# Layer-norm statistics from x's blocks instead of loaded rows, short steps moved between VectorE and GpSimd, three score visits a group, in a fused pre-norm attention kernel

## The chip, the cores and the metric

The kernel runs on one NeuronCore of one Trainium2 chip. The metric is device time in microseconds (us), the median over runs of the whole program. The engines are called as the profile calls them: PE is TensorE's matmul, PEld its weight load, DVE is VectorE, ACT ScalarE, POOL GpSimd, SP the queue that issues the DMAs. Each engine works through its own queue strictly in the order in which the kernel wrote its instructions, and waits on semaphores where one needs another's result.

## What is computed

One layer of graph attention with a layer norm ahead of it, in fp32, for 128 graphs of 128 nodes with 768 features, 12 heads of 64:

```
h = relu((x - mean(x)) / sqrt(var(x) + 1e-5))          # over the 768 features
q, k, v = h@Wq + bq, h@Wk + bk, h@Wv + bv              # 768 x 768 each, split in 12 heads
scores = q @ k.T / 8 + beta * adj
scores = where(adj > 0, scores, -9e15)
out = x + merge_heads(softmax(scores) @ v)
```

About one entry in eight of adj is positive.

## The kernel before

**Groups and slices.** The 128 graphs go in 32 groups of 4. A group's projections come in three slices: `qk0` (q and k of the first six heads), `v`, and `qk1` (q and k of the other six). Group 0 computes them plainly. From group 1 on each slice is a fast matrix multiplication of a 2x3 by a 3x3 block matrix in 15 block products instead of 18 (the table `PRODUCTS`). Its left factors are the normalized activations, transposed (`A00` to `A12`), and ten sums of them (`S0` to `S14`, in `SUMS_A`); its right factors are weight blocks and sums of these, prepared once in group 0, stored in HBM, and streamed in again in every group through a ring of six tiles (`load_T`), except ten that stay resident. Each of the 45 products of a group is 14 matmuls of 128x64 by 128x128 in pairs (28 instructions in the trace, line 681).

**Banks, evictions, decodes.** PSUM is held as four pairs of banks. The 15 products of a slice form four chains (a to d): a chain takes one pair for all its products and accumulates in it, and its running sum is added into the result tiles after each product (`evict`, DVE, line 704; the first addition to a tile goes mostly over ACT, lines 716 and 724 to 726, since it also brings the bias). The next product of a chain waits for the eviction before it, and the pair is given back after the chain's last one. When a result tile has all its parts, `decode` (lines 739 to 742 for q and k, 750 to 754 for v) turns its seven blocks into the four wanted. A decode runs on POOL or on DVE as the table `DECODE` says.

**Attention.** For each pair of heads (`oc`, 0 to 5) there are: `scores` (64x64-tiled matmuls, line 776, into a pair of its own), `mask` (DVE, 789), `exp` (ACT, 798), `attend` (matmuls of 65 columns, line 855), `drain` (ACT, 885 and 887), `recip` (DVE, 824), `divide` (ACT, 836), `add` of the residual (904; DVE, but POOL for three of the last group's), and `send`. `attend` puts its matmuls one by one between those of the next product. A time at which PE leaves the products for one or more scores is called a visit here.

**Layer norm of a later group.** The group's four graphs are loaded twice. The first time row by row (`load_row`, 384 KB each, with nodes on partitions): ACT sums each row (521), scales it (522) and sums the squared deviations (523), DVE and POOL make the inverse deviation and the shift from that (530, 534, 535), and both go to HBM and come back in the block order (`turn_out` 539, `turn_in` 543). The second time x is loaded in blocks (`load_x`, 295), 32 nodes of a quarter of the features on each quarter of the partitions; ACT normalizes the blocks (`norm`, 560), DVE transposes them into the left factors (`to_hT`, 580), POOL completes these (`inner`, 590 to 592), DVE makes the ten sums (`sum_acts`, 585).

**Order.** From group 1 on the order is written out: one unit is the place of a product, 45 units are a group. `ORDER` gives the order of a slice's products, `EVICT` and `DECODE` the keys of evictions and decodes, `TABLE` those of all else (relative to the group whose work it is; negative keys lie in the group before). `slice_z` issues a product and then everything whose key lies below the next unit. Separate tables hold for the first groups (`FIRST`, `SECOND`) and the last (`LAST`). Two scores whose keys lie in the same unit are thus one visit.

Of the kernel before, what the change touches and what calls it, by code (L numbers as in the profile page):

```python
# [11 lines left out]
F32 = mybir.dt.float32  # L12
# [6 lines left out]
P = 128  # L19
# [13 lines left out]
def kernel(  # L33
# [77 lines left out]
ZORDER = (1, 0, 5, 2, 3, 7, 10, 11, 6, 13, 4, 9, 14, 8, 12)  # L111
QORDER = (4, 0, 1, 8, 2, 3, 5, 6, 7, 10, 9, 11, 13, 12, 14)
VORDER = (1, 0, 5, 3, 2, 10, 6, 7, 13, 4, 11, 9, 8, 12, 14)
LORDER = (1, 4, 0, 5, 8, 2, 3, 10, 6, 7, 13, 11, 9, 14, 12)
PORDER = (1, 0, 5, 2, 3, 10, 7, 6, 13, 11, 4, 9, 14, 8, 12)
XORDER = (1, 0, 5, 2, 3, 10, 6, 7, 13, 11, 4, 9, 14, 8, 12)
ORDER = {"qk0": (1, 0, 5, 2, 10, 3, 6, 7, 13, 11, 9, 4, 14, 12, 8), "v": (1, 0, 5, 2, 10, 3, 6, 7, 13, 11, 4, 9, 14, 8, 12), "qk1": (4, 1, 0, 8, 2, 5, 3, 6, 7, 10, 9, 13, 11, 12, 14)}
RING = 6
RESIDENT = (10, 12, 16, 21, 29, 33, 36, 39, 41, 42)
# [6 lines left out]
    (-103.105, 'row', 0), (-86.74, 'row_stats', 0), (-85.688, 'row', 1), (-78.233, 'row_stats', 1),  # L126
    (-76.202, 'row', 2), (-71.584, 'row_stats', 2), (-67.928, 'row', 3), (-64.453, 'row_stats', 3),
    (-54.853, 'moments'), (-53.424, 'load_x', 0, (0,)), (-50.853, 'load_x', 0, (1,)), (-49.522, 'powers'),
    (-51.725, 'load_x', 0, (2,)), (-49.052, 'turn_out'), (-49.398, 'load_x', 0, (3,)), (-46.515, 'turn_in'),
    (-40.942, 'norm', 0, 2, 4), (-41.357, 'norm', 0, 0, 2), (-40.317, 'norm', 1, 2, 4), (-39.199, 'norm', 1, 0, 2),  # L130
    (-37.336, 'turn', 'A01'), (-34.768, 'turn', 'A02'), (-35.86, 'turn', 'A00'), (-33.123, 'load_x', 1, (0,)),
    (-32.146, 'load_x', 1, (1,)), (-30.708, 'load_x', 1, (2,)), (-32.534, 'load_x', 1, (3,)), (-24.763, 'inner', 'A00'),
    (-24.393, 'norm', 2, 0, 2), (-25.315, 'norm', 2, 2, 4), (-23.262, 'norm', 3, 2, 4), (-23.244, 'norm', 3, 0, 2),
    (-23.578, 'inner', 'A01'), (-20.844, 'adj'), (-18.417, 'inner', 'A02'), (-20.599, 'turn', 'A11'),
# [4 lines left out]
    (5.399, 'sum', 'S5'), (8.41, 'sum', 'S14'), (9.857, 'sum', 'S11'), (17.129, 'scores', 0, 2),  # L139
    (17.594, 'mask', 2), (18.011, 'exp', 2), (17.884, 'scores', 0, 1), (20.163, 'mask', 1),  # L140
    (23.187, 'exp', 1), (23.44, 'scores', 0, 0), (24.691, 'mask', 0), (26.808, 'xo', 2),
    (29.787, 'exp', 0), (33.304, 'attend', 2), (34.708, 'drain', 2), (38.169, 'recip', 2),
    (37.453, 'attend', 1), (40.226, 'divide', 2), (40.335, 'xo', 1), (40.001, 'drain', 1),
    (40.047, 'attend', 0), (42.314, 'xo', 0), (41.101, 'drain', 0), (41.291, 'recip', 1),
    (42.019, 'add', 2), (43.363, 'send', 2), (41.655, 'recip', 0), (47.272, 'xo', 5),
    (42.336, 'divide', 0), (46.026, 'divide', 1), (47.4, 'add', 1), (49.422, 'send', 1),
    (47.396, 'scores', 1, 2), (47.912, 'mask', 5), (47.949, 'scores', 1, 0), (49.895, 'add', 0),
    (49.151, 'mask', 3), (51.424, 'send', 0), (50.757, 'exp', 5), (51.214, 'scores', 1, 1),
    (51.428, 'mask', 4), (56.184, 'xo', 4), (50.986, 'exp', 3), (52.741, 'attend', 5),
    (53.334, 'drain', 5), (53.605, 'recip', 5), (54.069, 'divide', 5), (54.524, 'attend', 3),  # L150
    (55.36, 'drain', 3), (57.434, 'recip', 3), (54.287, 'xo', 3), (57.116, 'add', 5),
    (58.808, 'send', 5), (52.838, 'exp', 4), (58.432, 'divide', 3), (57.867, 'attend', 4),
    (58.283, 'drain', 4), (58.872, 'recip', 4), (61.984, 'divide', 4), (63.775, 'add', 3),
    (69.353, 'add', 4), (70.997, 'send', 4), (72.651, 'send', 3),
)
FIRST = (
    (47.506, 'scores', 1, 2), (48.607, 'mask', 5), (50.338, 'xo', 5), (51.293, 'exp', 5),
    (48.854, 'scores', 1, 0), (49.931, 'mask', 3), (53.115, 'exp', 3), (50.06, 'scores', 1, 1),
    (52.234, 'mask', 4), (52.147, 'xo', 3), (55.733, 'exp', 4), (52.181, 'attend', 5),
    (53.448, 'drain', 5), (54.046, 'xo', 4), (53.711, 'recip', 5), (55.811, 'divide', 5),  # L160
    (55.187, 'attend', 3), (56.589, 'drain', 3), (58.071, 'recip', 3), (60.187, 'add', 5),
    (58.585, 'divide', 3), (58.053, 'attend', 4), (59.743, 'drain', 4), (60.118, 'recip', 4),
    (64.402, 'send', 5), (62.463, 'divide', 4), (61.794, 'add', 3), (62.914, 'add', 4),
    (63.456, 'send', 3), (67.258, 'send', 4),
)
SECOND = (
    (-15.32, 'sum', 'S6'), (-45.161, 'halve'),
)
SOONER = (
)  # L170
LAST = (
    (35.303, 'xo', 0), (31.635, 'xo', 1), (26.501, 'xo', 2), (32.505, 'attend', 2),
    (33.547, 'drain', 2), (33.554, 'recip', 2), (35.3, 'divide', 2), (35.121, 'attend', 0),
    (36.619, 'drain', 0), (35.991, 'add', 2), (37.63, 'recip', 0), (40.956, 'send', 2),
    (38.462, 'divide', 0), (39.644, 'attend', 1), (40.439, 'drain', 1), (38.622, 'add', 0),
    (41.811, 'scores_half', 3, 1), (40.516, 'recip', 1), (41.663, 'send', 0), (40.926, 'divide', 1),
    (41.938, 'scores_half', 5, 0), (42.905, 'attend_half', 3, 1), (43.277, 'out_half', 3, 1), (41.384, 'add', 1),
    (42.934, 'attend_half', 5, 0), (44.439, 'scores_half', 5, 1), (43.462, 'out_half', 5, 0), (44.118, 'send', 1),
    (45.949, 'scores_half', 4, 0),
)  # L180
DECODE = {
# [45 lines left out]
def direct(ctx, tc, x, adj, wq, bq, wk, bk, wv, bv, beta, out, bad):  # L227
# [62 lines left out]
    def load_x(G, r, parts=range(NB)):  # L290
        if parts[0] == 0:
            home_x(G, r)
# [1208 lines left out]
```

## Time and profile before

| | before |
|---|---|
| median of 3 runs | 2666.85 us (2665.64 to 2668.2) |
| span of the profiled execution | 2664.1 us |
| PE busy | 2644.1 us, 99% |
| DVE, ACT, POOL busy | 81%, 66%, 79% |
| DMA | 736.65 MB, mean 277 GB/s |

A row of the timeline has the start in us from the span's start, the length, the engine, the line, and the operation with what it writes and reads; "x28" joins as many neighbours. As matmuls overlap, time on PE is read from start to start. In the groups by line a row ends with busy us, mean ns of one, and the idle time of the engine ahead of them with what ended it. "issue" is a wait for nothing that the profile shows.

### The profile page before, as it was taken

Reading aid. Unit: us, or ns where it says so; the run is one execution under the profiler, and the core shown is the slowest. Engines: PE = TensorE matmul, PEld = TensorE weight load, DVE = VectorE, ACT = ScalarE, POOL = GpSimd, SP = SyncE. Lnnn points to the kernel's source line nnn. Section 1 sums busy time; section 2 is a strip of 40 time slices with the busy share of each in tenths; the row PEclk is TensorE's granted clock in tenths of the full one; section 3 lists DMA queues with packets and bytes.
Section 4 is the critical chain, followed back from the end, with each engine's and each line's share of the span. In section 5 each row is a group of like instructions: output and inputs, shape, how many; then the busy total and the mean of one; then the engine's idle time right before and its main releaser. Section 6 shows DMA issues by size and latency. Waiting matters only on the chain.

```text
span 2664.1 us, 121442 instructions
## 1 busy us (share of the span) xinstructions
PE 2644.1 (99%) x52041; PEld 2564.2 (96%) x52041; DVE 2165.8 (81%) x2702; ACT 1755.1 (66%) x4608; POOL 2097.8 (79%) x3043
## 2 busy tenths in 40 slices
PE   9999999999999999999999999999999999999998
PEld 8799999999999999999999999999999999999997
DVE  7878887878888788887788887888877888778876
ACT  2567766677666677666777666776667776667654
POOL 5877778877779777788777797777887777887774
PEclk9999999999999999999999999999999999999999
DMA  8899999998989999999999899999899898999885
GB/s 254 276 281 279 282 284 278 283 292 267 293 281 279 287 277 284 281 281 280 289 269 288 281 281 282 288 275 285 279 278 292 268 291 279 276 286 282 256 253 165
DMA packets 531572, 736.65 MB, mean 277 GB/s; under 512 B 106444, under 2 KB 371160, under 8 KB 531032
## 3 DMA queue, kind: packets, MB, share of 16 engines
q1 hardware_dynamic: 530384, 728.06, 88.5%
q8 instruction: 411, 6.73, 1.0%
q14 instruction: 129, 1.06, 0.1%
q10 hardware_dynamic: 648, 0.79, 0.1%
HBM read 662.22 MB, written 66.51 MB: 274 GB/s over the span
## 4 chain that ended last, share of the span: by engine, by line
PE 94%; DVE 1%; DMA 0%; issue 0%; ACT 0%; SPq 0%; DVEq 0%; ACTq 0%
PE pair L681 80%; PE pair L776 7%; PE pair L855 6%; PE pair L1048 1%; DVE home L704 0%; DMA x<-in_x_dram 0%; DMA T_qk<-kept_qk 0%; PE pair L926 0%; DVE e L789 0%; DVE prep_qk L403 0%; ACT e L836 0%; DVE res_qk L403 0%; PE pair L947 0%; DVE e L931 0%; ACT e L933 0%
## 5 line engine op out<-in xcount | busy, mean ns | idle before, releaser
L704 DVE TENSOR_TENSOR home<-home,pair 128x896 f32<-128x896 f32 x836 | 880.0, 1077 | 220.5 <-PE pair L681 179.8
L681 PE MATMUL pair<-sbig,T_qk 128*64 128x128 f32 x13020 | 827.6, 274 | 2.3 <-DVE home L704 1.2
L681 PEld LDWEIGHTS pair<-sbig,T_qk 128*64 128x64 f32 x13020 | 702.5, 137 | 19.9 <-issue 12.1
L739 POOL TENSOR_TENSOR home<-home 128x256 f32<-128x256 f32 x308 | 266.1, 864 | 320.0 <-DVE home L704 319.7
L681 PE MATMUL pair<-T_v,sbig 128*64 128x128 f32 x7812 | 457.8, 273 | 1.6 <-ACT home L716 0.6
L681 PE MATMUL pair<-A,T_qk 128*64 128x128 f32 x6944 | 445.6, 273 | 0.9 <-issue 0.9
L681 PEld LDWEIGHTS pair<-T_v,sbig 128*64 128x64 f32 x7812 | 430.7, 137 | 8.4 <-ACT e L836 4.8
L855 PE MATMUL pair<-v,e 128*64 128x65 f32 x6048 | 403.5, 221 | 0.0
L836 ACT ACTIVATE e<-e,sm 128x64 f32<-128x64 f32 x1512 | 381.7, 341 | 7.4 <-DVE sm L824 6.1
L681 PEld LDWEIGHTS pair<-A,T_qk 128*64 128x64 f32 x6944 | 384.6, 137 | 1.5 <-issue 1.5
L855 PEld LDWEIGHTS pair<-v,e 128*64 128x64 f32 x6048 | 362.2, 137 | 3.2
L724 ACT ACTIVATE home<-pair 128x640 f32<-128x640 f32 x340 | 240.6, 708 | 188.5 <-PE pair L681 187.2
L681 PE MATMUL pair<-sbig,res_qk 128*64 128x128 f32 x4340 | 312.3, 273 | 0.4
L742 POOL TENSOR_TENSOR home<-home 128x256 f32<-128x256 f32 x308 | 269.7, 876 | 24.1
L885 ACT ACTIVATE sm<-pair,tiny 128x8 f32<-128x8 f32 x189 | 50.8, 269 | 329.5 <-PE pair L855 329.5
L789 DVE SCALAR_TENSOR_TENSOR e<-pair,biasT 128x1024 f32<-128x1024 f32 x189 | 229.4, 1214 | 34.1 <-PE pair L776 33.0
L740 POOL TENSOR_TENSOR home<-home 128x256 f32<-128x256 f32 x308 | 228.2, 741 | 24.1
L681 PEld LDWEIGHTS pair<-sbig,res_qk 128*64 128x64 f32 x4340 | 238.0, 137 | 1.4 <-DVE home L704 1.3
L560 ACT ACTIVATE x<-x,block 128x192 f32<-128x192 f32 x480 | 222.6, 540 | 0.0
L726 ACT ACTIVATE home<-pair,bqk 128x128 f32<-128x128 f32 x680 | 214.3, 377 | 0.0
L798 ACT ACTIVATE e<-e 128x1024 f32<-128x1024 f32 x189 | 196.1, 1055 | 21.8 <-DVE e L789 14.0
L741 POOL TENSOR_TENSOR home<-home 128x128 f32<-128x128 f32 x308 | 175.6, 570 | 24.2
(208 smaller groups left out, 4401.6 us busy)
## 6 DMA issues: line engine op xcount, KB each, us to landing
T_qk<-kept_qk SPq DMA_DIRECT2D x713, 448.0 KB
T_v<-kept_v SPq DMA_DIRECT2D x372, 448.0 KB
xo<-in_x_dram SPq DMA_DIRECT2D x190, 256.0 KB
out_dram<-xo SPq DMA_DIRECT2D x189, 256.0 KB
x<-in_x_dram SPq DMA_DIRECT2D x248, 192.0 KB
sbig<-in_x_dram SPq DMA_DIRECT2D x116, 384.0 KB
kept_qk<-prep_qk SPq DMA_DIRECT2D x23, 448.0 KB
adj<-in_adj_dram SPq DMA_DIRECT2D x128, 64.0 KB
```

The costliest lines, as they stand in the source:

```text
L560: nc.scalar.activation(t, t, AF.Relu, bias=shift[G, n], scale=rstd[G, n])
L681: nc.tensor.matmul(p[q:q + HD, at, :], lhs[:, q:q + HD], rhs, start=(first and at % 4 == 0), stop=True, skip_group_check=True)
L704: nc.vector.tensor_tensor(t, t, p[:, 0:7], op)
L724: nc.scalar.activation(t[:, 0:5], p[:, 0:5], AF.Copy, scale=float(sign))
L726: nc.scalar.activation(t[:, at], p[:, at], AF.Identity, bias=bqk[:, of, oc:oc + 1], scale=float(sign))
L739: e.tensor_tensor(t[:, 1:4:2], t[:, 1:4:2], twice(5), ALU.add)
L740: e.tensor_tensor(t[:, 2:5:2], t[:, 2:5:2], twice(1), ALU.add)
L742: e.tensor_tensor(t[:, 0:7:6], t[:, 0:7:6], twice(2), ALU.add)
L789: nc.vector.scalar_tensor_tensor(e[:, :, at], ps[:, :, at], SCORE_CAP * ISCALE, bias[:, :, at], op0=ALU.min, op1=ALU.add)
L798: nc.scalar.activation(e, e, AF.Exp, scale=1.0 / ISCALE)
L836: nc.scalar.activation(o[:, r, b, 0:HD], pa[:, r, b, 0:HD], AF.Copy, scale=t[:, 1, r, b:b + 1])
L855: nc.tensor.matmul(pa[q:q + HD, 2 * g + i, :], k[:, q:q + HD], vt[G, "v", r, h // 4][:, 4 * g + h % 4, :], start=True, stop=True, skip_gro ...
```

## The change

**Statistics from the blocks.** `load_row`, `row_stats`, `moments`, `turn_out` and `turn_in` go. For two graphs at a time (r = 0, 1), DVE runs `bn_stats` on the blocks of x that are loaded anyway, 16 steps of 128x192 a group; the results go to HBM and come back with all four quarters of a node's features on every partition that needs them; seven short DVE steps combine them (`comb`), POOL takes the power (`powers`), now twice a group with 8 columns.

```diff
+    def bn(G, g):
+        for b in range(NB):
+            nc.vector.bn_stats(st_x[:, (g % 2) * NB + b, :], xg[G, g][:, b, :])
+    def stout(G, r):
+        t = turned[G, r] = dram.tile([SQ, NB, 2 * NB * 6], F32, name=f"turned_{G}_{r}")
+        nc.sync.dma_start(t.rearrange("i a s -> a i s"), st_x.rearrange("p m s -> p (m s)"))
+    def stin(G, r):
+        nc.sync.dma_start(back.rearrange("p a m s -> p (a m s)"), turned.pop((G, r)).rearrange(
+            "i a s -> i (a s)")[None].to_broadcast([NB, SQ, NB * 2 * NB * 6]))
+    def comb(G, r):
+        v = back.rearrange("p a m (h s) -> p a m h s", h=2)
+        total = stat.tile([P, 2, 2 * NB], F32, tag="total", name=f"total_{G}_{r}", bufs=1)
+        nc.vector.tensor_reduce(total[:, 0], v[:, :, :, :, 1].rearrange("p a m h -> p m a h"), AX.XY, ALU.add)
+        nc.vector.tensor_scalar(total[:, 0], total[:, 0], -0.125, None, op0=ALU.mult)
+        nc.vector.tensor_tensor(dev, v[:, :, :, :, 1], total[:, 0][:, None, :, None].to_broadcast([P, NB, 2 * NB, 2]), ALU.add)
+        nc.vector.tensor_tensor(dev, dev, dev, ALU.mult)
+        nc.vector.scalar_tensor_tensor(dev, v[:, :, :, :, 2], 2.0 / QD, dev, op0=ALU.mult, op1=ALU.add)
+        nc.vector.tensor_reduce(total[:, 1], dev.rearrange("p a m h -> p m a h"), AX.XY, ALU.add)
+        nc.vector.tensor_scalar(total[:, 1], total[:, 1], 0.125, EPS, op0=ALU.mult, op1=ALU.add)
```

**Who does what.** Four of the ten sums and three of the six adds of a group move from DVE to POOL; four decodes a group are on DVE where one was. `OPEN` can give a first eviction to DVE in part (1) or whole (2); of its entries two meet a first eviction in the new order: `('v', 2): 1`, which cuts an ACT step in two, and `('qk1', 10): 1`, which gives three of seven blocks to DVE. Three attentions a group (`oc` 0, 2, 4) are issued in one piece, not between the matmuls of the next product.

```diff
+ADD_POOL = (1, 4, 5)
+SUM_POOL = ('S7', 'S11', 'S1', 'S9')
+WHOLE = (0, 2, 4)
 DECODE = {
+    ('qk0', 0, 0): (3.197731, 'v'), ('v', 0, 0): (8.0, 'v'), ('v', 1, 1): (4.200223, 'v'), ('qk1', 0, 0): (4.769773, 'v'),
...
-        nc.vector.tensor_tensor(t, full[G, a], full[G, b], ALU.add if sign > 0 else ALU.subtract)
+        e = nc.gpsimd if name in SUM_POOL and G > 1 else nc.vector
+        e.tensor_tensor(t, full[G, a], full[G, b], ALU.add if sign > 0 else ALU.subtract)
...
-        between.append(attend_steps(G, oc, behind))
+        steps = attend_steps(G, oc, behind)
+        if (G or oc > 2) and oc in WHOLE:
+            for _ in steps:
+                pass
+        else:
+            between.append(steps)
```

**Three visits and new tables.** All of `ORDER`, `RESIDENT`, `TABLE`, `EVICT`, `DECODE` and `LAST` has new keys; the fifteen products of a slice stay. `FIRST`, `SECOND` and the slots of group 0 give way to `EARLY` and to `TABLE` itself, whose keys count in group 1 too. Assertions (`needs`, `did`) now state at build time what must have been issued before what; they issue nothing.

```diff
-ORDER = {"qk0": (1, 0, 5, 2, 10, 3, 6, 7, 13, 11, 9, 4, 14, 12, 8), "v": (1, 0, 5, 2, 10, 3, 6, 7, 13, 11, 4, 9, 14, 8, 12), "qk1": (4, 1, 0, 8, 2, 5, 3, 6, 7, 10, 9, 13, 11, 12, 14)}
+ORDER = {'qk0': (4, 1, 0, 8, 5, 2, 3, 10, 6, 7, 9, 11, 13, 12, 14), 'v': (4, 1, 8, 5, 10, 0, 3, 2, 7, 13, 6, 11, 9, 14, 12), 'qk1': (4, 1, 0, 8, 3, 5, 2, 10, 6, 7, 9, 13, 11, 12, 14)}
 TABLE = (
-    (17.129, 'scores', 0, 2), (17.884, 'scores', 0, 1), (23.44, 'scores', 0, 0),
-    (47.396, 'scores', 1, 2), (47.949, 'scores', 1, 0), (51.214, 'scores', 1, 1),
+    (18.989782, 'scores', 0, 2), (18.992782, 'scores', 0, 1), (18.995782, 'scores', 0, 0),
+    (49.992037, 'scores', 1, 2), (49.995037, 'scores', 1, 0), (55.18473, 'scores', 1, 1),
...
+    (-29.538203, 'bn', 3), (-29.183478, 'stout', 1), (-29.137527, 'stin', 1),
+    (60.668615, 'attend', 3), (61.942528, 'attend', 4),
 )
```

More of the change, by code (lines that the diff above doesn't have):

```diff
@@ L346, in raw_qk1_piece @@
         v = flat(0, RAW).rearrange("p (c i n) -> p c i n", c=NC, i=2)
+        needs("part", "qk0", n=27)
+        did("raw")
         a, i = at // 2, at % 2
@@ L670, in product @@
             banks[chain] = take()
+        needs("A", G, an)
+        assert not waiting.get(chain)
+        waiting[chain] = len(uses)
         bank = banks[chain]
@@ L769, in scores @@
         oc = 3 * u + j
+        if G:
+            needs("decode", G, u, j, n=2)
         ps = take()
@@ L1007, in put, with slice_z @@
         heapq.heappush(events, (at, named[0], f, args))
-    def slice_z(G, sl, todo):
+    def slice_z(G, sl):
+        assert not prep
         order = order_of(G, sl)
         base = 45 * G + 15 * ("qk0", "v", "qk1").index(sl)
-        name = {(1, "qk0"): "first", (NG - 1, "v"): "vlast", (NG - 1, "qk1"): "last"}.get((G, sl), sl)
+        own = f"{sl}_last" if G == NG - 1 else f"{sl}_{G}"
         for k, n in enumerate(order):
@@ new lines, in direct, with placed @@
+        "raw": lambda G, n: raw_qk1_piece(n), "home": ninth_home, "load_T": lambda G: load_T(), "scores_half": scores_half, "attend_half": attend_first, "out_half": out_half,
+    }
+    for at, name, G, *args in EARLY:
+        put(at, actions[name], G, *args)
+    inputs = ("load_x", "bn", "stout", "stin", "comb", "powers", "norm", "turn", "inner", "adj", "bias1", "square", "bias2", "bias3")
+    def placed(G, at, name, args):
+        if name == "scores":
+            u = args[0]
+        elif name in ("mask", "exp", "xo", "attend", "drain", "recip", "divide", "add", "send"):
+            u = args[0] // 3
+        else:
+            if G == 1 and name in inputs:
+                return False
+            if G == 1 and name == "sum" and args[0] in ("S1", "S9", "S10", "S2", "S6"):
+                return False
+            return G > 0
+        if G == NG - 1:
+            return not u and name == "scores"
+        return G > 0 or u == 1
```

397 lines of the change are left out of this document (211 added, 186 removed), and 55 rows, old and new, of tables (DECODE, EVICT, OPEN, TABLE).

## The prediction

> **What bounds the kernel now.** I read the page first, then the busy time by windows, the chain of waits in order of time, and PE's timeline around the stretches that the change moves.
>
> ```profile
> span 2664.1 us, 121442 instructions
> ...
> PE 2644.1 (99%) x52041; PEld 2564.2 (96%) x52041; DVE 2165.8 (81%) x2702; ACT 1755.1 (66%) x4608; POOL 2097.8 (79%) x3043
> ```
>
> PE (TensorE) works through the whole span. A window of 82 us in the middle shows every engine's share there; its columns are length, PE, weight loads, DVE, ACT, POOL, granted clock, DMA share, GB/s.
>
> ```profile
> 918.00:1000.00 82.00, 82.00 (x1673) 80.40 (x1670) 67.49 (x81) 55.63 (x146) 66.34 (x96) 1.00 0.92 281
> ```
>
> PE has no hole, at full clock. DVE is busy 82%, POOL 81%, ACT 68%, the DMA engines 92%. Not one of them holds PE up. The chain of waits agrees: its longest pieces are one and the same piece of PE work, once a group.
>
> ```profile
> 252.99 15.65 PE pair L681 x284
> ...
> 334.02 15.65 PE pair L681 x284
> ...
> 2527.99 15.65 PE pair L681 x284
> ```
>
> The first two are 81.03 us apart, the shortest group. From the first to the last are 28 groups in 2275.0 us, 81.25 each: some 0.22 us a group, 6.2 us in all, are irregular waits. So there is next to nothing to win by relieving another engine. Only less work on PE counts, and the danger is that a busier engine makes PE wait.
>
> **Part by part: the PE stream.** The products are the same fifteen per slice, in another order. What changes is how often PE leaves them for scores.
>
> ```profile
> 211.69 1.98 PE L776 MATMUL pair<-home 64*64 64x128 f32 x64
> 213.59 4.81 PE L681 MATMUL pair<-sbig,T_qk 128*64 128x128 f32 x84
> 218.23 1.70 PE L681 MATMUL pair<-A,T_qk 128*64 128x128 f32 x28
> 219.86 0.67 PE L776 MATMUL pair<-home 64*64 64x128 f32 x16
> 220.34 0.62 PE L776 MATMUL pair<-sbig 64*64 64x128 f32 x16
> 220.89 1.86 PE L681 MATMUL pair<-sbig,T_qk 128*64 128x128 f32 x30
> ```
>
> Read start to start, since ends overlap. A visit with two scores (x64) lasts 213.59 - 211.69 = 1.90; one with a single score (x32) 220.89 - 219.86 = 1.03. A score more costs 0.87, so 0.16 of a visit is not for scores. The product ahead of the single visit lasts 219.86 - 218.23 = 1.63, where products elsewhere take 1.53:
>
> ```profile
> 1001.87 1.70 PE L681 MATMUL pair<-sbig,res_qk 128*64 128x128 f32 x28
> 1003.40 1.70 PE L681 MATMUL pair<-A,T_qk 128*64 128x128 f32 x28
> ```
>
> Another 0.10 is thus paid on entry: 0.26 us a visit, whatever it holds. Before, a group has four visits: keys 17.129 and 17.884 fall into one slot, 23.44 into another, 47.396 and 47.949 into one, 51.214 alone. After, 18.990 to 18.996 are one slot with three scores, 49.992 and 49.995 one, 55.185 alone: three. The first half's visit is saved in groups 1 to 31; in group 0 three visits of the second half become two. 32 x 0.26 = 8.3 us less on PE, the one term on the path. As bounds: 32 x 0.16 = 5.1 if entry is paid in any case, 8.3 if the third score is never late.
>
> Three of the six attentions are now issued whole, not between the products' matmuls. The last group has one that stands alone:
>
> ```profile
> 2644.34 0.93 PE pair L947 x32
> ```
>
> 0.93 us for 32 instructions. PE's stream holds those 32 either way, and nothing in this row suggests that standing together costs more: zero, with the neighbouring products as cover for its weight loads; without that cover the bound is the 0.10 of a change of shape, three times a group, 9 us in all.
>
> **Part by part: the other engines.** Prices, as busy time and mean of one:
>
> ```profile
> L704 DVE TENSOR_TENSOR home<-home,pair 128x896 f32<-128x896 f32 x836 | 880.0, 1077 | 220.5 <-PE pair L681 179.8
> ...
> L904 DVE TENSOR_TENSOR xo<-xo,e 128x512 f32<-128x512 f32 x186 | 161.8, 870 | 0.1
> ...
> L585 DVE TENSOR_TENSOR sbig<-sbig,A 128x896 f32<-128x896 f32 x93 | 118.5, 1274 | 1.0
> ...
> L534 POOL TENSOR_TENSOR row<-verow,nhalf 128x4 f32<-128x4 f32 x30 | 30.8, 1028 | 0.0
> ...
> L464 DVE BATCH_NORM_STATS2 st<-x 128x6 f32<-128x192 f32 x16 | 4.4, 343 | 2.6 <-DMA x<-in_x_dram 2.6
> ...
> L904 POOL TENSOR_TENSOR xo<-xo,e 128x512 f32<-128x512 f32 x3 | 3.6, 1185 | 9.1 <-ACT e L836 9.1
> ```
>
> A decode (four steps from L739 on) on DVE, start to start, and beside it a sum that met POOL at work:
>
> ```profile
> 1012.32 1.60 DVE L585 TENSOR_TENSOR sbig<-A,A 128x896 f32<-128x896 f32 x1
> ...
> 1018.84 0.65 DVE L739 TENSOR_TENSOR home<-home 128x256 f32<-128x256 f32 x1
> ...
> 1021.96 1.34 DVE L585 TENSOR_TENSOR sbig<-sbig 128x896 f32<-128x896 f32 x1
> ```
>
> 3.12 us. And two on POOL, the second beside that sum of 1012.32:
>
> ```profile
> 1010.09 0.73 POOL L739 TENSOR_TENSOR home<-home 128x256 f32<-128x256 f32 x1
> ...
> 1012.93 1.58 POOL L739 TENSOR_TENSOR home<-home 128x256 f32<-128x256 f32 x1
> ...
> 1017.14 0.72 POOL L739 TENSOR_TENSOR home<-home 128x256 f32<-128x256 f32 x1
> ```
>
> 2.84 us undisturbed, 4.21 where it meets DVE; I take 3.1, nearer the first.
>
> DVE per group: now 67.49 x 81.03 / 82 = 66.7. Added: 16 statistics steps at 4.4 / 16 = 0.275, 4.4; 14 short steps of the combination, between nothing beyond their issue and the 0.34 of a statistics step, I take 0.2, 2.8; three more decodes at 3.12 (a v decode priced like a qk one, an estimate), 9.4; half an eviction where the split puts three of seven blocks on DVE, 0.5. Gone: four sums at 1.27, 5.1; three adds at 0.87, 2.6. Net +9.4, 76.1 of the new period of 80.77: 94%. Bounds: 73.3 with the short steps free, 78.1 with all at 0.34.
>
> POOL per group: now 65.6. Gone: three decodes, 9.3. Added: three adds at 1.19, 3.6; four sums of 896 columns, 896 / 512 x 1.185 = 2.07 each, 8.3; the power step twice on eight columns for once on four, between +1.0 and +3.1, I take 2. Net +4.6, 70.2: 87%.
>
> ACT loses all row passes, and with 68% now is not the limit. SP loses four row loads of 384 KB a group; in their place stand two stores and two broadcast loads of some 0.25 MB together. 281 GB/s x 81.03 us is 22.8 MB a group, so the DMA share falls from 0.92 to about 0.87. SP's second broadcast load (key -29.138) stands right behind its store (-29.183), and so waits for the statistics step and the store's landing; queued behind it are the T loads, and PE waits for those only once the ring of six is used up: about five products, 7.6 us. I price it at zero.
>
> Nothing of this is on the path while every eviction comes in time. The place to look is the triple visit, since it wants three of the four pairs of banks at once. Take t = 0 at the end of v's first product. DVE has the last qk0 eviction (1.08) and two short first evictions (about 0.5 each) to do, at 2.1 a third that waits for v's second product, then the new decode and the eviction that frees the last pair. PE ends the second product at 1.53 + 2 x 0.93 = 3.4 (two attentions fall there), the fourth at 6.45, and wants the third pair at 6.45 + 0.10 + 2 x 0.87 = 8.3. DVE: 3.4 + 0.5 = 3.9, decode 7.0, eviction 8.1. It fits, by 0.2 us.
>
> One rule is weighed here. A DVE step with two SBUF inputs and a POOL step slow each other in the rows above (1.60 beside 1.58). The Trainium skill (SBUF — State Buffer, Who interferes with whom) says why: the two share one port pair, whoever starts first holds it for its whole instruction and the other is blocked. By that rule the sums moved to POOL free DVE, and their long instructions hold DVE's remaining two-input steps; it gives no time by itself.
>
> **The rivals.** First, **the third score waits**: DVE is some 0.26 us late at every triple visit, against the cover of 0.2. Then each group loses what it saved, and the time stays at 2666.85. For it: that cover is the smallest that I find, and durations spread (1.27 mean, 1.60 at worst for a sum). Against: DVE runs ahead wherever it need not wait for PE.
>
> Second, slower: **DVE becomes the bound** because POOL's long steps hold it up. It decides once collisions add 80.77 - 76.1 = 4.7 us a group. Seven new long POOL steps (four sums, three adds) that each hold a DVE step for 0.75 us, a bit more than half of 1.185, add 5.3: 81.4 a group, 0.63 over, 31 x 0.63 = 19.5 us; the visits saved are still inside the 80.77, so the time is 2666.85 - 8.3 + 19.5 = 2678. For it: 94% of a strict queue, in which a late step makes every eviction behind it late. Against: POOL's moved work replaces DVE's own sums, which collided before too. The Trainium skill's rule (SBUF — State Buffer, Who interferes with whom) is this mechanism: by it a hold could last the whole 2.07 of a sum.
>
> Third, **more than the visits**: with the DMA share down, the irregular 6.2 us vanish too: 2652.4.
>
> **How the numbers follow.** The profiled execution spans 2664.1; the median of the runs is 2666.85, 2.75 above, which I keep. 2664.1 - 8.3 + 2.75 = 2658.5 is the forecast. About 0.2%, 5.3 us, is what a measurement here can tell from no change. The forecast with its neighbours (2652 to 2661.5, the third rival within it at 0.08) has 0.53; the wait at the third score, with all between 2661.5 and 2672, has 0.21; DVE as the bound, from 2672 to about 2700, has 0.26. The range reaches from the third rival, 2652, past the second, 2678, to 2688, a loss of 1.0 us a group. The likeliest case alone has 2652 to 2661.5.
>
> **What would show it.** Right: three L776 groups a period on PE's timeline, one of x96 that lasts 0.16 + 3 x 0.87 = 2.77; a shortest period of 80.77; DVE at 94% and POOL at 87% with PE without holes; no L521 or L523 on ACT; DMA share 0.87. The first rival shows as an x96 visit of 3.0 or more, with PE released by DVE's eviction. The second shows as PE idle before L681, released by DVE, all over the period, DVE near 99%, and POOL's 128x896 sums or the DVE steps beside them well over 2.07 and 1.27. I am wrong altogether if the groups' period grows with DVE below 94%, or if the visits' price stays in the products around them.

## The result and the profile after

The changed kernel takes 2725.14 us (median of 4 runs, 2722.34 to 2729.7), the one before 2666.9 beside it: a ratio of 1.0221, 95% interval 1.0209 to 1.0233. The forecast was 2658.5, faster. It is 58 us slower and 67 us off the forecast, outside the range.

The page of the changed kernel, its span, its engines, and the chain that ended last by engine and by line:

```profile
span 2725.0 us, 121572 instructions
...
PE 2652.7 (97%) x52041; PEld 2577.7 (95%) x52041; DVE 2367.0 (87%) x3822; ACT 1494.9 (55%) x3977; POOL 2175.8 (80%) x2884
...
PE 78%; DMA 7%; SPq 7%; DVE 4%; issue 2%; POOL 1%; ACT 0%; ACTq 0%; DVEq 0%; POOLq 0%
PE pair L753 67%; PE pair L858 5%; PE pair L947 5%; DMA x<-in_x_dram 5%; SPq L661 4%; SPq L327 2%; DVE sbig L554 1%; DVE home L777 1%; DMA T_v<-kept_v 1%; DMA kept_v<-prep_v 0%; DMA sbig<-in_L_gnn_Wk_dram 0%; SPq L479 0%; DMA kept_qk<-prep_qk 0%; DMA sbig<-in_x_dram 0%; POOL prep_v L419 0%
```

No engine got fuller than it should: DVE 87%, POOL 80%, and PE has lost its 99%. But 22% of the last chain is no longer PE, and the names in it are a load of x, SP's issue of `adj` (L661) and of x (L327), and the statistics (L554). The window that the prediction showed of before:

```profile
918.00:1000.00 82.00, 80.06 (x1633) 78.77 (x1629) 71.84 (x116) 46.98 (x125) 67.69 (x90) 1.00 0.87 258
```

PE now has 1.94 us of holes where it had none, at full clock, with DVE busy 88%. What PE and DVE waited for between 205 and 2560 us, some 28 groups (us in all, times, longest). A wait of PE before L753 that ended by "issue" stands in the middle of a product and is called mid-product below:

```profile
DVE sbig L554 <- DMA x<-in_x_dram: 30.5, 25, 2.4
...
DVE sbig L554 <- issue: 10.0, 8, 2.3
...
PE pair L947 <- DVE home L777: 25.3, 23, 2.3
...
PE pair L753 <- issue: 18.0, 24, 1.9
...
DVE biasT L668 <- DMA adj<-in_adj_dram: 4.4, 7, 1.4
```

Once in nearly every group, at the same place: DVE waits for x at the statistics, and PE for an eviction at an attention. The eight waits of L554 put down to "issue", and one of 2.4 us put down to a load of T_v, are waits for x too: all 34 end within 0.2 us of a landing of x by the semaphores of its loads, 42.9 us in all. Here it is in one group, in the timeline of SP, then of DVE, then of PE, and in the chain of that stretch:

```profile
1057.38 0.87 SPq L327 DMA_DIRECT2D x<-in_x_dram  x2
...
1058.88 4.57 SPq L661 DMA_DIRECT2D adj<-in_adj_dram  x4
1063.49 3.71 SPq L327 DMA_DIRECT2D x<-in_x_dram  x2
```

```profile
1070.04 1.14 DVE L554 BATCH_NORM_STATS2 sbig<-x 128x6 f32<-128x192 f32 x4 [1.18 <-DMA x<-in_x_dram]
1071.09 0.18 DVE L910 RECIPROCAL sm<-sm 128x8 f32<-128x8 f32 x1
1071.19 1.03 DVE L777 TENSOR_TENSOR home<-home,pair 128x896 f32<-128x896 f32 x1
```

```profile
1071.09 0.39 PE L753 MATMUL pair<-T_v,sbig 128*64 128x128 f32 x4
1072.38 0.45 PE L947 MATMUL pair<-v,e 128*64 128x65 f32 x8 [0.90 <-DVE home L777]
```

```profile
1063.49 5.57 DMA x<-in_x_dram
```

Read it backwards. PE wants to start an attention at about 1071.3 and needs a pair. The eviction that frees the pair stands on DVE behind the statistics step. That step stood at the head of the queue for 1.18 us because the last two parts of x were not there: SP asked for the first of them only at 1063.49, since `adj` (4.57 us of issue) lay in between, and it landed 5.57 us later, at 1069.06. The last part was asked for at 1066.6, once SP was through with the one ahead, and landed by its semaphore at 1069.96; the step starts at 1070.04. The statistics themselves cost 1.1 us for four steps, just as priced; the wait ahead of them was not priced.

The visits, on PE's timeline at the triple visits of two neighbouring groups:

```profile
2578.82 0.67 PE L858 MATMUL pair<-home 64*64 64x128 f32 x16
...
2581.60 0.66 PE L753 MATMUL pair<-T_v,sbig 128*64 128x128 f32 x8
...
2659.37 2.85 PE L858 MATMUL pair<-home 64*64 64x128 f32 x96
```

One visit of 96 instructions lasts 2581.60 - 2578.82 = 2.78 us, forecast 2.77. And the period between these two, the last of the kernel, is 2659.37 - 2578.82 = 80.55: the only one below 81.3 in this trace, and the only one with no next group behind it whose x and `adj` have to come in. All others lie between 81.32 and 85.49.

A second reading goes by the products' matmuls: numbering the 39,060 of them (group 1 on) in order in both traces and comparing the start of the same number. At the 600th, in group 1, the changed kernel is 7.9 us behind, but by then it has done one score more, as the triple visit comes before the place that this score has in the kernel before. At the 800th, with the same scores and attentions done in both, it is 6.9 behind; at the last, 60.7. So about 7 us are lost once at the start, and 54 in the groups.

### The profile page after: what moved, and what is told of

Read it like the earlier page. It is cut to its first block, busy times and chain, and to the rows that moved or that the text cites. A ratio compares the mean times of both kernels' runs of the same rounds, so it can differ in the third digit from the quotient of the medians.

```text
span 2725.0 us, 121572 instructions
## 1 busy us (share of the span) xinstructions
PE 2652.7 (97%) x52041; PEld 2577.7 (95%) x52041; DVE 2367.0 (87%) x3822; ACT 1494.9 (55%) x3977; POOL 2175.8 (80%) x2884
## 4 chain that ended last, share of the span: by engine, by line
PE 78%; DMA 7%; SPq 7%; DVE 4%; issue 2%; POOL 1%; ACT 0%; ACTq 0%; DVEq 0%; POOLq 0%
PE pair L753 67%; PE pair L858 5%; PE pair L947 5%; DMA x<-in_x_dram 5%; SPq L661 4%; SPq L327 2%; DVE sbig L554 1%; DVE home L777 1%; DMA T_v<-kept_v 1%; DMA kept_v<-prep_v 0%; DMA sbig<-in_L_gnn_Wk_dram 0%; SPq L479 0%; DMA kept_qk<-prep_qk 0%; DMA sbig<-in_x_dram 0%; POOL prep_v L419 0%
## 5 line engine op out<-in xcount | busy, mean ns | idle before, releaser
L753 PE MATMUL pair<-sbig,T_qk 128*64 128x128 f32 x12152 | 762.3, 273 | 5.6 <-ACT e L980 3.6
L753 PEld LDWEIGHTS pair<-sbig,T_qk 128*64 128x64 f32 x12152 | 683.7, 137 | 12.6 <-issue 7.9
L753 PE MATMUL pair<-T_v,sbig 128*64 128x128 f32 x7812 | 492.4, 274 | 12.8 <-issue 11.9
L753 PEld LDWEIGHTS pair<-T_v,sbig 128*64 128x64 f32 x7812 | 439.5, 137 | 22.9 <-issue 18.5
L753 PE MATMUL pair<-A,T_qk 128*64 128x128 f32 x6076 | 379.2, 274 | 7.7 <-issue 4.5
L753 PEld LDWEIGHTS pair<-A,T_qk 128*64 128x64 f32 x6076 | 343.8, 137 | 15.6 <-issue 12.0
L947 PE MATMUL pair<-v,e 128*64 128x65 f32 x6048 | 316.5, 222 | 33.1 <-DVE home L777 27.5
L753 PE MATMUL pair<-sbig,res_qk 128*64 128x128 f32 x5208 | 335.8, 273 | 0.0
L947 PEld LDWEIGHTS pair<-v,e 128*64 128x64 f32 x6048 | 292.1, 138 | 42.5 <-issue 37.5
L595 POOL TENSOR_TENSOR rstd<-total,nhalf 128x8 f32<-128x8 f32 x60 | 101.8, 1697 | 268.4 <-DVE total L584 268.4
L753 PEld LDWEIGHTS pair<-sbig,res_qk 128*64 128x64 f32 x5208 | 287.5, 137 | 0.0
L819 POOL TENSOR_TENSOR home<-home 128x256 f32<-128x256 f32 x274 | 224.9, 821 | 53.8 <-DVE home L777 53.3
L753 PE MATMUL pair<-T_v,A 128*64 128x128 f32 x4340 | 263.7, 273 | 0.2 <-ACT home L792 0.2
L609 ACT ACTIVATE x<-x,shift,rstd 128x192 f32<-128x192 f32 x492 | 228.4, 542 | 48.2 <-POOL shift L596 28.9
L820 POOL TENSOR_TENSOR home<-home 128x256 f32<-128x256 f32 x274 | 231.5, 845 | 21.5
L822 POOL TENSOR_TENSOR home<-home 128x256 f32<-128x256 f32 x274 | 229.2, 836 | 21.5
L753 PEld LDWEIGHTS pair<-T_v,A 128*64 128x64 f32 x4340 | 243.8, 137 | 1.7 <-ACT home L792 0.3
```

The costliest lines, as they stand in the source:

```text
L609: nc.scalar.activation(t, t, AF.Relu, bias=shift[G, n], scale=rstd[G, n])
L753: nc.tensor.matmul(p[q:q + HD, at, :], lhs[:, q:q + HD], rhs, start=(first and at % 4 == 0), stop=True, skip_group_check=True)
L819: e.tensor_tensor(t[:, 1:4:2], t[:, 1:4:2], twice(5), ALU.add)
L820: e.tensor_tensor(t[:, 2:5:2], t[:, 2:5:2], twice(1), ALU.add)
L822: e.tensor_tensor(t[:, 0:7:6], t[:, 0:7:6], twice(2), ALU.add)
L947: nc.tensor.matmul(pa[q:q + HD, 2 * g + i, :], k[:, q:q + HD], vt[G, "v", r, h // 4][:, 4 * g + h % 4, :], start=True, stop=True, skip_gro ...
```

## The experiments

Theory A: a DVE step that reads what a DMA brings, placed before the data have landed, stops DVE's queue, and the evictions behind it stop PE. Theory B (the prediction's slower rival): DVE has too much work, or is blocked by POOL. Theory C: the burst of loads holds up PE's own instructions. Theory D (from e4 on): moving a load only makes the next transfer the late one. Between keys, one unit is a product: 1.53 us of PE where nothing else falls into it, 80.55 / 45 = 1.79 on average. The diffs of the tables show the changed keys alone, without the rest of their lines. Where an expectation gives a larger figure for a wait than the views here (33.8, 46.5, 19.4, 12.5 us), it is not of this stretch and view.

**e1, x's parts first.**

```diff
-    (-35.732659, 'adj'), (-34.736351, 'load_x', 1, (3,)), (-34.397373, 'load_x', 1, (1,)),
+    (-37.89, 'load_x', 1, (3,)), (-37.88, 'load_x', 1, (1,)), (-35.732659, 'adj'),
```

> The changed kernel, with the last two parts of the second x load issued right behind the first two, ahead of the adj load. Theory A (the statistics step on DVE stands at the head of its queue waiting for x, and the evictions behind it hold an attention's bank): the wait goes, and with it most of the 33.8 us that PE loses ahead of attentions; 2692 to 2700 us. Theory B (DVE simply has too much work, or is blocked by POOL's long steps): DVE's work is the same, 2725 us. Theory C (most of the loss is PE's own instruction supply, held up by a burst of DMA traffic): the same bytes at nearly the same place, 2715 to 2725 us, with the waits in the middle of products unchanged.

Measured 2754.75 us, ratio 1.034 (1.0321 to 1.0359): slower still, a miss. Its waits in the same stretch:

```profile
DVE biasT L668 <- DMA adj<-in_adj_dram: 42.1, 25, 3.6
...
PE pair L947 <- DVE home L777: 26.6, 20, 2.8
...
DVE sbig L554 <- DMA x<-in_x_dram: 1.5, 2, 1.0
```

The wait for x is gone as meant (30.5 to 1.5 us), but `adj` now comes later, and the step that reads it (L668, key `bias1`, a transpose of `adj`; the expectations call it the bias sum), which stands ahead of the statistics, waits in their place, longer.

**e2, the statistics later.** `bn`, `stout`, `stin`, `comb`, `powers` and three norms of the second half go 2 to 7 units later (not the eight to twelve that the expectation names), the loads stay.

```diff
-    (-32.064071, 'bn', 2), (-29.538203, 'bn', 3), (-29.137527, 'stin', 1), (-21.424467, 'comb', 1),
+    (-24.95, 'bn', 2), (-23.5, 'bn', 3), (-22.0, 'stin', 1), (-17.9, 'comb', 1),
```

> The changed kernel, with the loads where they are, but the second pair of statistics steps eight to twelve product units later (and the store, the load back, the combination and the normalizing of these two graphs after them). Theory A: x has landed by then, 2692 to 2700 us. Theory B: DVE's work is only moved to another stretch, 2715 to 2725 us. Theory C: 2715 to 2725 us, waits in the middle of products unchanged.

Measured 2805.53 us, ratio 1.0515 (1.0491 to 1.0539), a miss again:

```profile
PE pair L753 <- DVE home L777: 65.2, 24, 4.1
DVE total L578 <- DMA sbig<-turned: 52.1, 27, 3.2
```

Now it is the first step of the combination (L578) that heads DVE's queue, four units behind the load that brings the statistics back.

**e3, statistics of other data.** For graphs 2 and 3 of each group, the statistics are taken of a resident activation tile instead of x: the same steps at the same places, without a load to wait for. Half of the graphs are normalized with statistics that are not theirs.

```diff
-            nc.vector.bn_stats(st_x[:, (g % 2) * NB + b, :], xg[G, g][:, b, :])
+            src = xg[G, g][:, b, :] if g < 2 else full[G, "A00"].rearrange("p z n -> p (z n)")[:, 3 * P:3 * P + QD]
+            nc.vector.bn_stats(st_x[:, (g % 2) * NB + b, :], src)
```

> The changed kernel, whose second pair of statistics steps reads a tile of activations that DVE itself wrote earlier, in place of x (the statistics of half of the graphs are thus of other data). Same steps, same place, no wait for the x load. Theory A: 2692 to 2700 us. Theory B: 2725 us, since DVE's busy time is the same. Theory C: 2715 to 2725 us.

Measured 2673.35 us, ratio 1.0028 (1.0017 to 1.0038): 52 us come back, more than theory A had expected. Page, and the window 918 to 1000:

```profile
PE 2638.4 (99%) x52041; PEld 2572.2 (96%) x52041; DVE 2366.2 (88%) x3822; ACT 1493.1 (56%) x3977; POOL 2177.7 (81%) x2884
```

```profile
918.00:1000.00 82.00, 82.00 (x1664) 80.66 (x1662) 74.02 (x119) 47.66 (x129) 68.35 (x89) 1.00 0.88 266
```

DVE and POOL do the same work as in the changed kernel (2366.2 and 2177.7 us against 2367.0 and 2175.8), DVE is even fuller in the window, and PE has no hole. Theory B falls; the wait for x was the loss. Theory C in its strong form falls as well, since all loads stayed where they were.

**e6, adj and the bias at the places of before.** The load of `adj` and the four bias steps get the keys that they have in the kernel before.

```diff
-    (-35.732659, 'adj'), (-32.095103, 'bias1'), (-24.111881, 'square'), (-20.687762, 'bias2'),
+    (-20.844, 'adj'), (-16.854, 'bias1'), (-14.905, 'square'), (-14.031, 'bias2'),
```

> The changed kernel, with the adj load and the four bias steps at the keys that the kernel before had (the load 15 units later). Theory A: the x parts are issued some 4.6 us sooner, the statistics steps find x there, 2692 to 2700 us. Theory B: two DVE steps fewer ahead of the evictions in that stretch, but more later: 2715 to 2725 us. Theory C: adj's small pieces leave the burst, the waits in the middle of products go down by half or more from some 20 us; with A true as well 2675 to 2685 us, with A false 2705 to 2715 us.

Measured 2813.8 us, ratio 1.0566 (1.0536 to 1.0596), the third miss. DVE waits 86.2 us for `adj`, once a group:

```profile
1044.29 0.71 DVE L668 STREAM_TRANSPOSE biasT<-adj 128x512 f32<-128x512 f32 x1 [3.67 <-DMA adj<-in_adj_dram]
1044.93 1.05 DVE L777 TENSOR_TENSOR home<-home,pair 128x896 f32<-128x896 f32 x1
```

The same keys in the kernel before gave 0.3 us of such waits in all: a slot is safe only together with the queues around it. The next four give the loads their lead, together or one by one.

**e4, both loads early.** As e1, and `adj` some 12 units ahead of the bias sum, behind the first half's statistics in SP's queue. **e5** moves `adj` alone.

```diff
-    (-35.732659, 'adj'), (-34.736351, 'load_x', 1, (3,)), (-34.397373, 'load_x', 1, (1,)),
+    (-44.5, 'adj'), (-37.89, 'load_x', 1, (3,)), (-37.88, 'load_x', 1, (1,)),
```

> Both late loads move: x's parts 3 and 1 ahead of adj as in e1, and adj's load to slot -44.5, some 12 products ahead of the bias sum that reads it. Theory A, carried on from e1 and e2 (any DVE step at the head of its queue whose data were asked for only two to four products before holds the evictions behind it): neither the statistics of x nor the bias sum is late any more, and the time comes to that of the run with other data for the statistics, 2665 to 2680 us. Theory D (the move of a load only makes the next transfer the late one, here the statistics' way out and back or the T loads behind adj on SP): 2690 to 2750 us, with total <- DMA sbig or PE <- DMA T in the waits. Theory C (PE's instruction supply suffers from the traffic wherever it stands): above 2700 us.

> Only adj's load moves, from between x's parts to slot -44.5. Its issue takes SP 4.57 us a group, and x's last two parts stand behind it, so they are asked for about 4.5 us sooner, with their own slots the limit (two products behind the first parts). Theory A: most of the 1.2 us a group at L554 goes, and the waits behind it: 2672 to 2695 us, a little above the run with both loads early. Theory D: 2700 to 2750 us, another transfer is the late one. Theory C: no better than 2700 us.

e4: 2667.37 us, ratio 1.0003 (0.9994 to 1.0013). e5: 2683.34 us, ratio 1.0048 (1.003 to 1.0067). Both as theory A says; D falls for them. e4's waits and its window 918 to 1000:

```profile
DVE sbig L554 <- DMA x<-in_x_dram: 7.7, 12, 1.9
PE pair L753 <- issue: 6.3, 9, 1.6
...
PE pair L947 <- DVE sbig L777: 1.2, 1, 1.2
PE pair L947 <- DVE home L777: 0.7, 1, 0.7
```

```profile
918.00:1000.00 82.00, 82.00 (x1674) 80.97 (x1672) 74.79 (x120) 48.39 (x130) 69.69 (x92) 1.00 0.90 267
```

Of PE's waits at attentions 1.9 us are left, of the mid-product ones a third. Nothing of the change's arithmetic was undone, only three loads were asked for sooner: 58 us. In e5 the wait at L554 is 14.9 us, half of the changed kernel's, since x's last parts no longer stand behind `adj` and are still late.

**e7, x's parts first and the bias sum later**, from -32.1 to -26, with `adj` where it was.

```diff
-    (-32.095103, 'bias1'), (-24.111881, 'square'),
+    (-26.0, 'bias1'), (-23.0, 'square'),
```

> x's parts first as in e1, adj's load where it was, and the bias sum that waited in e1 put off from slot -32.1 to -26 (its square from -24.1 to -23). Theory A: the bias sum then finds adj there, and nothing else heads DVE's queue early: 2668 to 2690 us, and L668's wait for adj falls from 46.5 us in e1 to under 10. Theory D: the late adj load also puts the statistics' way out and back and the T loads later, and the time stays above 2710 us.

Measured 2671.73 us, ratio 1.0017 (1.0003 to 1.0031). No wait at L668 is left. Moving the step that reads, or the load that feeds it, does nearly the same.

**e8**, e3 with `adj` early (half of the statistics not their own, as there):

> As the run whose statistics of every second pair of graphs are of other data (half the graphs' statistics are not their own, the output differs), with adj's load early too. That run still had 7.4 us of the bias sum's wait for adj, and 19.4 us of mid-product waits. Theory A: the 7.4 us go, 2662 to 2670 us. Theory C: the mid-product waits that stay there are of the x load's burst and not of adj's, so the time stays at 2670 to 2678 us with the same mid-product waits.

Measured 2664.14 us, ratio 0.9988 (0.9978 to 0.9997): 9 us less than e3, where the bias sum had still waited 7.4 us for `adj`. Even with hardly a wait for x (0.6 us) this order of work comes only 3 us below the kernel before.

**f1, the start.** By the products' matmuls, e4 is 6.9 us behind at the 600th (5.8 at the 800th, with equal work done) and 0.1 ahead at the end. At the start, PE waits for a drain and for an eviction, whose order goes back to the statistics of group 2 at the head of DVE's queue. f1 puts those statistics four units later (e4 otherwise); **h1** leaves them and takes the reciprocal behind them forward.

```diff
+OVER = {(2, 'bn', 0): 43.35, (2, 'bn', 1): 43.36, (2, 'stout', 0): 43.6, (2, 'stin', 0): 44.6, (2, 'comb', 0): 47.6,
```

> Both loads early as in the run that came to 2667 us, and for group 2 alone, whose x is loaded while the first products of group 1 run, the statistics of x stand some four products later, behind two reciprocals of group 0's attentions instead of ahead of them. Counted by products, that run is 6.9 us behind the kernel before at the 600th product of the slices and 0.1 us ahead at the end: the start costs 7 us and the groups give them back. Theory S (the same kind of wait, once: x lands 5.70 us after its issue, the statistics at the head of DVE's queue, a reciprocal behind, the divide behind that on ACT, and PE waits 3.6 and 1.6 us for pairs): 3 to 6 us go, 2661 to 2664 us, ratio to before 0.9975 to 0.999. Rival (the start is slow for the order of its products and attentions, not for that wait): no change, 2666 to 2669 us.

> As the version with adj early and x's parts spread (2667 us), and at the start the first reciprocal of group 0's attentions goes ahead of the statistics that wait for x, with its divide a product and a half sooner; the statistics stay. Theory S (the reciprocal behind the waiting statistics held a divide, a drain and so a pair that PE needs): the 3.6 us at the start go, perhaps the 1.6 us behind them too, 2661 to 2665 us, and at the 600th product it is 1 to 4 us behind the kernel before instead of 6. Rival (the first group's order and its tables' DMAs set the start): another wait takes its place, as it did when the statistics were moved, 2666 to 2669 us, and still 6 us or more behind.

f1: 2672.26 us, ratio 1.0013 (1.0001 to 1.0026), outside both of its ranges. h1 (built on f4, below): 2665.98 us, ratio 0.9994 (0.9986 to 1.0003). Neither recovers the start: they are 8.3 and 5.6 us behind at the 600th matmul (7.2 and 4.4 at the 800th). PE's waits from 100 to 175 us, in e4, in f1 (lines one higher) and in h1:

```profile
PE pair L753 <- ACT e L980: 3.6, 1, 3.6
PE pair L753 <- ACT home L804: 1.6, 1, 1.6
```

```profile
PE pair L754 <- DMA T_qk<-kept_qk: 4.0, 1, 4.0
PE pair L859 <- DVE sbig L778: 2.0, 1, 2.0
```

```profile
PE pair L753 <- DVE sm L910: 2.5, 1, 2.5
PE pair L753 <- ACT home L804: 2.5, 1, 2.5
```

Each time another wait is the last. Theory S falls. A second part of the loss is the granted clock, which the kernel before has at 1.00 all through the start. In e4 it is halved, beginning within the wait of 3.6 us (first a window as above, then two rows of PE):

```profile
127.50:137.80 10.30, 7.12 (x64) 6.57 (x66) 5.27 (x14) 10.13 (x35) 1.85 (x2) 0.50 0.97 240
```

```profile
133.94 3.25 PE L753 MATMUL pair<-A,T_qk 128*64 128x128 f32 x28 [1.57 <-ACT home L804]
136.98 2.09 PE L753 MATMUL pair<-sbig,T_qk 128*64 128x128 f32 x28
```

A product takes 136.98 - 133.94 = 3.04 us there, not 1.53. PE works 7.1 of the 10.3 us, so some 3.5 are lost to the clock; from group 1's first product to the 800th matmul its waits are 5.7 us, 2.9 in the kernel before. Together that is about the 5.8 that e4 is behind. h1 has no stretch at half clock and loses its 4.4 us by waits alone. What makes these waits in group 1 (its weight sums are made by POOL just then, and its order is new) stays open.

**f2, the triple visit split** (e4 otherwise).

```diff
-    (18.995782, 'scores', 0, 0),
+    (21.5, 'scores', 0, 0),
```

> Both loads early, and the third score of the triple visit (j = 0 of the first half) put off by two products, so that it is a visit of its own again: 30 visits more. The prediction's price of 0.26 us a visit (0.16 of switching, 0.10 of entry) gives 7.8 to 8.1 us: 2674 to 2677 us, shortest period between groups up by 0.26. Rival: only the switch counts, 0.16 us, 2672 us. Rival: the visit's price is covered by the waits that are there anyway: 2667 to 2669 us.

Measured 2682.6 us, ratio 1.0055 (1.0041 to 1.0069): 15 us more than e4, not 8. PE's timeline:

```profile
1063.86 0.67 PE L858 MATMUL pair<-home 64*64 64x128 f32 x16
...
1066.12 3.28 PE L753 MATMUL pair<-T_v,sbig 128*64 128x128 f32 x56 [0.28 <-ACT home L792]
...
1070.86 1.10 PE L858 MATMUL pair<-home 64*64 64x128 f32 x32
1071.89 1.31 PE L753 MATMUL pair<-T_v,sbig 128*64 128x128 f32 x20
```

The double visit takes 1066.12 - 1063.86 = 2.26 us with a wait of about 0.35 at its end (a double visit without one takes 1.91 elsewhere), the single one 1.03, and 0.10 is paid once more on entry. Without the wait that is 1.91 + 1.03 + 0.10 = 3.04 against the triple's 2.78: 0.26, the prediction's price. But the product behind a visit is longer too: in the prediction's rows three of them last 218.23 - 213.59 = 4.64 us, and 3 x 1.53 is 4.59, so 0.05 more are paid on leaving, and a visit costs 0.31. The shortest period bears this out: 81.21 us here, 80.55 in e4, so 0.66 = 0.31 for the visit and 0.35 for the wait. ACT's first eviction ends that wait, and in e4, where the third score runs on for another 0.9 us, none shows. Thirty times 0.66 would be 20 us; why 15 were measured is not resolved.

**f3, no attention whole** (e4, with two drains one or two units later).

```diff
-WHOLE = (0, 2, 4)
+WHOLE = ()
```

> Both loads early, and the three attentions that run whole (0, 2 and 4) are laid between a product's matmuls again, as the kernel before has all six (two drains go one or two products later for it). The prediction priced this at nothing: 2665 to 2669 us and the shortest period stays at 80.55 us. Rival: the 0.22 us by which the shortest period came out below the 80.77 us predicted are of the whole attentions: the period is 80.77 again, and the time 6 to 7 us longer, 2672 to 2675 us.

Measured 2744.68 us, ratio 1.0283 (1.0269 to 1.0297), which neither theory had. PE waits 33.0 us for a sum on DVE and 24.2 us for a drain ahead of the scores: the later drains hold pairs, and the order around them no longer fits. It says nothing on the price. The traces of two other kernels do: in the kernel before, a product with an attention in it takes 2.46 us from its start to that of the next (160 of them), and in e4 a product with a whole attention behind it takes 1024.46 - 1022.00 = 2.46:

```profile
1022.00 1.70 PE L753 MATMUL pair<-sbig,T_qk 128*64 128x128 f32 x28
1023.53 1.10 PE L947 MATMUL pair<-v,e 128*64 128x65 f32 x32
1024.46 1.70 PE L753 MATMUL pair<-sbig,T_qk 128*64 128x128 f32 x28
```

**f4, x's parts a unit apart** (`adj` early, first statistics two units later).

```diff
-    (-37.938599, 'load_x', 1, (0,)), (-37.90816, 'load_x', 1, (2,)), (-34.736351, 'load_x', 1, (3,)), (-34.397373, 'load_x', 1, (1,)), (-32.064071, 'bn', 2),
+    (-37.938599, 'load_x', 1, (0,)), (-37.0, 'load_x', 1, (2,)), (-36.1, 'load_x', 1, (3,)), (-35.2, 'load_x', 1, (1,)), (-30.0, 'bn', 2),
```

> adj's load early, and x's four parts of the second load about a product apart (from slot -37.9 to -35.2) instead of four at once, with the first statistics two products later. Theory C, kept for the small part: PE's waits in mid-product (12.5 us with both loads early) are its instruction packets held up by the burst of x's load, so a thinner burst takes a third to a half of them away, 2661 to 2665 us. Theory A: the last part is asked for only three products ahead of the statistics, so the wait at the head of DVE's queue comes back in part: 2672 to 2690 us. Neither: 2666 to 2669 us.

Measured 2667.39 us, ratio 1.0 (0.9991 to 1.0009): no gain. In the one profiled execution (span 2658.4) PE's mid-product waits were fewer, but its 11 runs spread from 2660.14 to 2674.18, so this does not show that a thinner burst helps.

**h3, the mechanism in the kernel before.** One key of it, nothing of the change:

```diff
-    (-16.854, 'bias1'),
+    (-19.0, 'bias1'),
```

> The kernel before, with one key changed: the bias sum that reads adj stands 1.8 products behind adj's load (slot -19.0) instead of 4.0 (-16.9). Nothing of the change is in it. Theory A (a DVE step that heads its queue before its data have landed holds the evictions behind it, whatever the step is): about 3 us of wait a group, some of it past the pairs' reserve, 2690 to 2750 us, with biasT <- DMA adj in the waits. Rival (only the changed kernel, with DVE at 87 to 94 per cent, has no reserve; at 81 per cent a wait is made good): 2667 to 2675 us.

Measured 2745.03 us, ratio 1.0282 (1.0262 to 1.0303). Its waits and one place in DVE's and in PE's timeline:

```profile
DVE biasT L605 <- DMA adj<-in_adj_dram: 76.3, 28, 4.2
...
PE pair L681 <- DVE home L704: 58.3, 28, 3.6
```

```profile
1103.19 0.71 DVE L605 STREAM_TRANSPOSE biasT<-adj 128x512 f32<-128x512 f32 x1 [2.02 <-DMA adj<-in_adj_dram]
1103.83 3.04 DVE L704 TENSOR_TENSOR home<-home,pair 128x896 f32<-128x896 f32 x3
```

```profile
1104.93 1.75 PE L681 MATMUL pair<-res_v,A 128*64 128x128 f32 x28 [1.37 <-DVE home L704]
```

A step of 0.7 us, moved forward by two units, costs the kernel before 79 us (up to 17 of them over the clock, see the last section), with DVE busy 79% overall. The rival (that a less busy DVE makes it good) falls. This is a mechanism of strict queues, not of the new statistics.

## Why the prediction was wrong

**The step that failed** is in the part on the other engines: "16 statistics steps at 4.4 / 16 = 0.275, 4.4", put into DVE's busy time, and then "Nothing of this is on the path while every eviction comes in time", looked for at the triple visit alone. The new steps were costed as work. They are also waits: the statistics of each group's second pair of graphs read x, which SP was still asking for behind `adj`, and DVE stood 42.9 us at the statistics for x. The row with their price even named it (2.6 us of idle time, released by the load of x). Queued behind them were a reciprocal and the eviction that frees the pair of an attention. e3 (52 us back without that wait), e4 (58 us back with the loads early) and h3 (79 us lost by one such step in the kernel before) show this.

**PE's term had the right sign and the wrong size, and e4's gain came near it by chance.** The triple visit takes 2.78 (2.77 forecast), but a visit costs 0.31 and not 0.26 (f2), and the shortest period came out at 80.55, not 80.77. The 81.03 of the kernel before was free of waits, as the prediction took it: several of its groups come to 81.02 or 81.03, and between 205 and 2560 us PE waits 1.5 us in all, the most of it here:

```profile
PE pair L681 <- issue: 1.3, 5, 0.4
```

So PE's work fell by 0.48 a group, some 15 us in 31: 0.31 is the visit, and 0.17 comes from four places of the old order where a product or a visit is 0.02 to 0.05 longer than others like it, for a reason that no run tested. Of this e4 keeps 5.9 us from the 800th matmul to the end, since PE waits 8.2 us between 205 and 2560 us where it had waited 1.5. That this lies near the 8.3 forecast is luck.

**Not priced: the start.** In the first groups every version with the change is 3 to 7 us behind by the 800th matmul. With the forecast's 8.3 that alone would have left next to no difference, and e4 shows none.

**Right, and not on the path:** DVE at 74.79 of 82 us in e4 (91%, forecast 94%), POOL at 69.69 (85%, forecast 87%); no wait of PE at the triple visit's scores, so the cover of 0.2 us held; whole attentions at nothing (f3); the statistics' way back (L568) behind its store kept PE from no T load but once (0.9 us). The DMA share, forecast at 0.87, is 0.90 in e4; the changed kernel has 0.87 only because its period is longer.

**The rivals.** The slower one gave a loss of the right sign by the wrong mechanism: it asked for DVE near 99%, and DVE was below 94% with the period longer, which the prediction itself named as the sign of being altogether wrong. The Trainium skill (SBUF — State Buffer, Who interferes with whom) says that a DVE step with two SBUF inputs and a POOL step that reads SBUF contend for one shared port pair, an exclusive lock; here DVE and POOL are fuller in e3 and e4 than in the changed kernel (DVE 74.02 and 74.79 of 82 us against 71.84) and PE has no holes in that window, so that rule does not decide this case. The third score's rival did not occur, and neither did the one with no irregular waits left: e4 has more of them than the kernel before.

## What to carry to other kernels

Before a step that reads a DMA's result goes into a strict queue, work out when its data land (where the issue stands in its own queue, the issue time of what is ahead of it, then the landing) and name what is queued behind it; busy time says nothing of this. If a moved load or step only makes the next one late, give all of them their lead together: e1, e2 and e6 each made it worse, e5 got 42 of the 58 us back, e4 all. And compare two traces by the same numbered piece of work, so that a loss at the start is not spread over the steady state.

## What the hardware showed beside this

The loads in question took 5.57 us (x, in the changed kernel), 5.22 (`adj`, e6) and 5.14 (the statistics' way back, e2) from issue to landing, so some three and a half products of PE; four issues of `adj` alone held SP for 4.57 us in the changed kernel.

PE also waited in the middle of products for nothing that the profile names ("issue"), up to 1.9 us at a time, 18.0 us in the changed kernel, 10.6 in e3, 6.3 in e4. The DMA packets of the traces tell what it was. One queue carries instructions, 16 KB a packet, one packet in about 6.5 us:

```profile
q8 instruction: 412, 6.75, 1.0%
```

Every one of these waits (24 in the changed kernel, 13 in e3, 9 in e4, 6 in the kernel before) ends 1.2 to 1.7 us after the end of such a packet, so PE was waiting for its own instructions. They fall at a place that moves back by about one matmul a group. That bursts of loads are what delays the packets, as theory C has it, was only argued, and f4 did not settle it.

A long wait of PE can cost more than its length. Between 205 and 2560 us the granted clock stood at 0.50 for 34 us in h3, 72 in e2, 79 in e6 and 7 in the changed kernel, in stretches of 3.4 or 6.8 us, and never in e4 and the kernel before. That is at most 17, 36, 39 and 3 us of these runs' losses. That the waits bring it on is read from the runs in which it stands, and was not tested; h1's two waits of 2.5 us went by without it.
